# Fold of Wq and Wk by block products, three more two-level products, and modifier's first layer summed in PSUM

## Chip, cores and metric

The kernel runs on one core of one Trainium2 chip, in float32. The metric is the device time of one execution in microseconds (us). A core has a matrix engine (TensorE, PE in the profile, with PEld for its weight loads), a vector engine (VectorE, DVE), a scalar engine (ScalarE, ACT), a general one (GpSimd, POOL) and a queue engine (SyncE, SP) that issues transfers. Each has a queue of its own and works through it in order. Matmuls write to PSUM, which has eight banks of 128 x 512 floats; SBUF holds all else.

## The reference

Four sequences x of 512 tokens and 512 features go through attention, two multilayer perceptrons and a small adapter. Cut to what is computed:

```python
q, k, v = x @ Wq, x @ Wk, x @ Wv
attn = softmax(q @ k.T * 512 ** -0.5)
attn_out = (attn @ v) @ Wp + bp
cms_out = gelu(attn_out @ cW1 + cb1) @ cW2 + cb2 + one_hot(codes)   # 512 -> 2048 -> 512
modifier = gelu(concat(attn_out, cms_out) @ mW1 + mb1) @ mW2 + mb2  # 1024 -> 2048 -> 512
h = clip(x + cms_out + modifier, 0, 1)
up = gelu(h @ W_down[s] + b_down[s]) @ W_up[s] + b_up[s]            # 512 -> 256 -> 512, s by sequence
out = layernorm(h + up) * ln_w[s] + ln_b[s]
```

## The kernel before

**Folded weights.** x Wq (x Wk)ᵀ is x (Wq Wkᵀ) xᵀ, so the kernel first makes w_qk = Wq Wkᵀ and, during the first attention, w_vp = Wv Wp. Wq and Wk are transposed by PE (`transposed`, L409, matmuls L414), copied out of PSUM in turn by DVE (L107) and ACT (L111), and multiplied by `product` (L423, matmuls L428): 16 matmuls of 512 columns. `block_weights` (L449) also makes the sums of w_qk's blocks on DVE as the products end.

**Block products.** Everything behind the fold is multiplied in the form of Strassen and Winograd: of a product of 2 x 2 blocks only seven block products are made instead of eight, from sums of blocks of either operand. They are numbered 1 to 7; a left operand has the sums s1 to s4, a right one t1 to t4. At one level a product saves an eighth of PE's columns; at two levels each of the seven is again made of seven, and another eighth goes. What it costs are additions of results on DVE. Two helpers do these:

- `seven` (L554) keeps the sums in PSUM: products 1, 5 and 6 open banks, 7 and 4 go on accumulating onto the bank of 6, 3 onto the one that DVE's sum y was written to, 2 onto that of 1. In between DVE adds in place (`add`, L509, instruction line L510), so PE waits for DVE inside one group: product 7 waits for `add(y, x, c15)`, product 4 for `add(v, x, c15)`. ACT copies product 1 out as c1 (L575).
- `inner` (L847) gives every product a bank of its own; ACT copies the first (L871), and DVE adds each of the other six out of PSUM (`plus`, L864), seven additions in all.

**Stages.** Sequences go in two pairs. A pair goes through attention (`small_product` L657 with matmuls L664, `pair_product` L595 with matmuls L600), through cms' first layer (`c1_layer`, L1000) and second layer (`second_layer`, L1154, matmuls L1180), through modifier's first layer (`m1_layer`, L1081, matmuls L1096) and second layer, and the adapters. Pair 0's adapters (matmuls L1279, L1288, L1300) are made in steps between the products of pair 1's cms first layer; pair 1's are made in its last layer and behind it. In cms' first layer products 1 and 5 are at two levels (`c1_two_level`, L955, matmuls L979), the other five at one (matmuls L1030). In modifier's first layer all are at two, by `inner`, in two halves g of the output, with `combine_first` (L898) adding the outer seven together on DVE and calling gelu. Both second layers are at two levels, by `inner`.

**Sums of operands.** The inner sums of token operands (`token_sums` L183, instruction line L190, four subtractions a product) are DVE's, made one product ahead. The sums of weights are POOL's: `expansion` (L355) and `late_expansion` (L368) load weights, add blocks (L178 to L181, L298) and store the sums to memory; SP's queue fetches them again into four weight slots, `wslot`. The main program calls a few steps of these generators between products (`steps`, L402), so POOL goes through them in that order, ahead of PE. Late expansion, for modifier's second layer, runs beside pair 0's modifier first layer, two steps per product.

**Small constants.** `constants` (L485 to L505) turns codes and adapter numbers into a one-hot column table (`target`) and row numbers for the gathers (`ex`, `idx_d`, `idx_u`): some 36 DVE instructions of 1 to 8 elements a partition, called in the first attention after w_vp.

**Order.** A scheduler orders the instructions of each engine by the kernel's dependences and a model of their costs; those in `tc.keep_in_program_order` stay in the order of the program on their engine. `second_operands` (L1121) makes the outer sums of a second layer's operand (2048-element subtractions on DVE) as the first layer ends.

## Time and profile before

| | us |
|---|---|
| three runs, median (lowest to highest) | 1199.15 (1198.18 to 1199.61) |
| the profiled execution | 1199.55 |
| its span | 1197.8 |
| PE busy / idle in the span | 1173.2 / 24.6 |
| DVE busy | 891.0 |
| ACT busy | 292.5 |
| POOL busy | 475.3 |

The stages by PE's work in that span: fold 0 to 25.2, attention of pair 0 to 147 and of pair 1 to 255.4, cms' first layer of pair 0 to 348.2 and second to 433.0, modifier's first layer to 606.8 and second to 691.4; then the same for pair 1: 816.6, 901.2, 1070.7 and 1163.9, and the last adapters to 1197.8. The mean granted clock of PE is 0.994.

In the lists of the trace a line such as `PE sum L664 <- DVE sum L510: 4.1, 1, 4.1` reads: PE, at line 664, waited for DVE's line 510, 4.1 us in all, once, the longest 4.1. In the order of time a line has its start, its length, the engine, the line of the kernel, the operation, its output and inputs, and the count of records. A float32 matmul leaves two records.

### The profile page before, as it was taken

To read this page: it belongs to the slowest core of one execution; us is meant where nothing else is said; L and a number is where in the kernel's file an instruction comes from. 1 tells how busy PE (TensorE), PEld (TensorE's weight loads), DVE (VectorE), ACT (ScalarE), POOL (GpSimd) and SP (SyncE) were. 2 spreads that over 40 slices of the span, in tenths; PEclk is the share of its full clock that TensorE was granted. 3 is DMA by queue.
4 is the path that set the end of the run, shared out by engine and by line. 5 is a ranking of instruction groups with operands and counts; after the bars stand their busy time and mean duration, and the time that the engine had idled before them with its cause. 6 is when DMAs were issued, how large, how long until landed. Compare 5 with 4: busy or idle time off the path is not lost.

```text
span 1197.8 us, 13100 instructions
## 1 busy us (share of the span) xinstructions
PE 1173.2 (98%) x4785; PEld 893.2 (75%) x4785; DVE 891.0 (74%) x1234; ACT 292.5 (24%) x535; POOL 475.3 (40%) x517
## 2 busy tenths in 40 slices
PE   8989999999999999999999999999999999999996
PEld 5468548747468888878888857447888888888872
DVE  2755565477789867798799837679895588699947
ACT  3215234426520000012210037461000002230014
POOL 5779999988910048880000532210000010124015
PEclk9999999999999999999999999999999999999998
DMA  8844586699636587886747553142744454675601
GB/s 299 298 154 176 192 321 235 220 386 369 259 111 242 179 276 306 298 287 228 233 163 282 185 184 132 44 141 106 279 143 172 180 206 172 211 245 183 231 1 70
DMA packets 78368, 251.50 MB, mean 210 GB/s; under 512 B 7348, under 2 KB 34016, under 8 KB 63456
## 3 DMA queue, kind: packets, MB, share of 16 engines
q1 hardware_dynamic: 54768, 149.96, 35.4%
q0 software_dynamic: 20736, 89.17, 21.2%
q10 hardware_dynamic: 2800, 11.54, 2.4%
q8 instruction: 38, 0.62, 0.2%
q14 instruction: 26, 0.21, 0.1%
HBM read 185.63 MB, written 65.01 MB: 209 GB/s over the span
## 4 chain that ended last, share of the span: by engine, by line
PE 92%; DVE 5%; ACT 1%; issue 1%; DMA 0%; DVEq 0%
PE i L1180 28%; PE i L1096 26%; PE c L1030 11%; PE sum L600 8%; PE sum L664 7%; PE sum L979 3%; PE prod_ps L428 2%; PE down_ps L1288 2%; PE tr_ps L414 2%; PE up_ps L1300 2%; DVE slot L190 1%; DVE hidden L510 1%; PE res_ps L1279 1%; DVE part L864 1%; DMA wide<-in_L_cond_Wq 0%
## 5 line engine op out<-in xcount | busy, mean ns | idle before, releaser
L1096 PE MATMUL i<-slot,wslot 128*128 128x256 f32 x1184 | 262.0, 380 | 2.3 <-DVE part L864 2.3
L1096 PEld LDWEIGHTS i<-slot,wslot 128*128 128x128 f32 x1184 | 225.1, 190 | 33.6 <-issue 2.4
L1180 PE MATMUL i<-slot,wslot 128*128 128x256 f32 x896 | 202.5, 379 | 0.0
L1180 PEld LDWEIGHTS i<-slot,wslot 128*128 128x128 f32 x896 | 170.4, 190 | 23.0
L871 ACT COPY first<-i 128x256 f32<-128x256 f32 (+1 forms) x56 | 26.8, 478 | 540.4 <-PE i L1180 280.7
L1180 PE MATMUL i<-hidden,wslot 128*128 128x256 f32 x576 | 132.2, 379 | 0.0
L864 DVE TENSOR_TENSOR part<-i,part 128x512 f32<-128x512 f32 (+1 forms) x156 | 90.9, 591 | 42.9 <-PE i L1096 26.2
L1180 PEld LDWEIGHTS i<-hidden,wslot 128*128 128x128 f32 x576 | 109.6, 190 | 16.0 <-issue 1.4
L893 ACT ACTIVATE hidden<-hidden,bias 128x512 f32<-128x512 f32 x128 | 85.2, 716 | 69.6 <-DVE hidden L510 69.5
L1030 PE MATMUL c<-slot,wslot 128*128 128x512 f32 x224 | 97.3, 592 | 0.0
L1030 PEld LDWEIGHTS c<-slot,wslot 128*128 128x128 f32 x224 | 42.5, 190 | 53.1 <-issue 50.4
L1251 POOL DMA_INDIRECT slot<-in_L_cond_W_down,idx_d x12 | 15.4, 1283 | 149.8 <-PE i L1180 88.5
L1251 POOL DMA_INDIRECT slot<-in_L_cond_b_up,idx_e x3 | 4.3, 1423 | 174.1 <-PE i L1096 173.5
L190 DVE TENSOR_TENSOR slot<-hidden,slot 128x1024 f32<-128x1024 f32 x48 | 58.4, 1218 | 0.3
L190 DVE TENSOR_TENSOR slot<-hidden 128x1024 f32<-128x1024 f32 x48 | 58.4, 1217 | 0.0
L864 DVE TENSOR_TENSOR part<-i,first 128x512 f32<-128x512 f32 (+1 forms) x62 | 36.3, 588 | 29.1 <-PE i L1096 16.6
L510 DVE TENSOR_TENSOR sum<-sum,wslot 128x512 f32<-128x512 f32 x48 | 33.4, 697 | 32.5 <-PE sum L600 17.6
L664 PE MATMUL sum<-hidden,wslot 128*128 128x256 f32 x224 | 53.1, 389 | 4.1 <-DVE sum L510 4.1
L510 DVE TENSOR_TENSOR hidden<-c,hidden 128x512 f32<-128x512 f32 x64 | 43.4, 688 | 15.5 <-PE c L1030 14.3
L284 POOL DMA_DIRECT2D slot<-in_L_cond_mW x24 | 17.9, 751 | 90.2 <-DVE slot L190 89.2
L664 PEld LDWEIGHTS sum<-hidden,wslot 128*128 128x128 f32 x224 | 43.4, 195 | 10.5 <-DVE sum L510 4.5
L510 DVE TENSOR_TENSOR hidden<-part,hidden 128x2048 f32<-128x2048 f32 x20 | 47.4, 2370 | 0.5
(301 smaller groups left out, 1990.5 us busy)
## 6 DMA issues: line engine op xcount, KB each, us to landing
wslot<-m_kept SPq DMA_DIRECT2D x48, 1024.0 KB, 6.5
wslot<-m_kept SPq DMA_DIRECT2D x36, 512.0 KB, 4.7
wslot<-c_kept SPq DMA_DIRECT2D x16, 1024.0 KB, 6.3
slot<-in_L_cond_mW POOLq DMA_DIRECT2D x24, 512.0 KB, 7.6
wslot<-in_L_cond_mW SPq DMA_DIRECT2D x24, 512.0 KB, 6.7
slot<-in_L_cond_cW POOLq DMA_DIRECT2D x16, 512.0 KB, 5.4
wslot<-in_L_cond_cW SPq DMA_DIRECT2D x32, 256.0 KB, 4.9
m_kept<-wide POOLq DMA_DIRECT2D x6, 1024.0 KB, 7.0
```

The costliest lines, as they stand in the source:

```text
L190: i = eng.tensor_tensor(out_, one, two, ALU.subtract)
L414: nc.tensor.transpose(ps[d][:, c * P : (c + 1) * P], get(c)[:, d * P : (d + 1) * P], ident)
L510: nc.vector.tensor_tensor(dst, a, b, ALU.add)
L600: nc.tensor.matmul(ps, lhsT=lhs[p][:, c, r * P : (r + 1) * P], rhs=rhs[p][:, c, :], start=(first_ and c == 0), stop=(c == 1), skip_group_c ...
L664: nc.tensor.matmul(v[:, j, :], lhsT=lhs[p][:, c, j * P : (j + 1) * P], rhs=rhs[p][:, c, :], start=(first_ and j == 0 and c == 0), stop=(c ...
L864: nc.vector.tensor_tensor(dst, ps, other, ALU.add)
L871: nc.scalar.copy(c1, p1)
L893: nc.scalar.activation(block[:, t, :], block[:, t, :], AF.Gelu, bias=bias_c[:, 8 * half + t : 8 * half + t + 1],)
L979: nc.tensor.matmul(halves_of(ps)[:, j, :], lhsT=a[g][:, at_[q], j * P : (j + 1) * P], rhs=rhs[q][:, 0, :], start=(first_ and j == 0), stop ...
L1030: nc.tensor.matmul(ps, lhsT=lhs(c, t), rhs=one_level[p][:, c, :], start=(c == 0), stop=(c == 1),)
L1096: nc.tensor.matmul(out_ps[:, j, :], lhsT=a[j][q][:, c, :], rhs=now[q][:, c, :], start=(c == 0), stop=(c == 1),)
L1180: nc.tensor.matmul(ps[:, :256], lhsT=a[k // 2][q][:, k % 2, :], rhs=now[q][:, k, :], start=(k == 0), stop=(k == 3),)
```

## The change

1. The fold of Wq and Wk goes from `product` to `small_product` (28 matmuls of 256 columns, `folded`). The sums of the operands' blocks are made by DVE from the transposes in PSUM (`left_from_psum`, `right_from_psum`), and ACT makes all copies of the transposes. It works in `wslot[0]`, `wslot[1]` and `slot[0]`.
2. `constants` goes from DVE to POOL, between the first weights' expansion and the rest; three gathers of adapter biases, which need it, stand behind it in POOL's queue.
3. In the last pair's cms first layer products 2, 6 and 7 are also at two levels. Their weight sums are made by POOL at the end of late expansion (`expand_c1_late`), the inner sums of their operands and two of the outer additions by POOL too. The steps of pair 0's adapters are called inside the products (`beside`) instead of between them. Late expansion goes at three steps per product.
4. Modifier's first layer goes from `inner` and `combine_first` to `seven`, with the outer additions of each product in its `keep`.
5. `second_operands`, except for pair 0's cms layer: half of the first outer sum is made by ACT copies with a factor of −1 and a transfer that POOL issues and that adds to what stands at its destination (`accum_op`), and one subtraction goes from the first layer's end to the second layer's start.

```diff
@@ late_expansion
-        yield from expand_all(m2_units, slot[6:8], (flat(mod[0]), flat(mod[1]), slot[0]), None)
+        spaces = (flat(mod[0]), flat(mod[1]), slot[0])
+        quarters = lambda tiles: [t[:, at : at + 1024] for t in tiles for at in (0, 1024)]
+        begin, rest = expand_c1_late(quarters(slot[6:8]), quarters(spaces[:2]))
+        yield from expand_all(m2_units, slot[6:8], spaces, None, begin)
+        yield from rest
@@ expand_c1_late, for units (p, u) of p in (2, 6, 7), u in 0, 1
+                weight_sums(
+                    raw[:, 0, 0], raw[:, 0, 1], raw[:, 1, 0], raw[:, 1, 1],
+                    *(to[:, k] for k in range(4)),
+                )
+                if i + 4 < len(units):
+                    load(i + 4)
+                nc.gpsimd.dma_start(out=c1_inner[p, u], in_=sums[i % 4])
+                yield
@@ expansion
         yield from expand_c1(1, lambda: load_raw(cW2, False, 0, slot[4:6]))
+
+        constants()
@@ constants
-            nc.vector.tensor_scalar(target[:, b, :], pos, code[:, b : b + 1], None, ALU.is_equal)
-            nc.vector.tensor_add(target[:, b, :], target[:, b, :], cb2_c)
+            nc.gpsimd.tensor_scalar(target[:, b, :], pos, code[:, b : b + 1], None, ALU.is_equal)
+            nc.gpsimd.tensor_add(target[:, b, :], target[:, b, :], cb2_c)
...
@@ the fold
-    transposed(chunks(wq), big[4])
-    transposed(chunks(wk), big[5])
-    lhs_qk = block_weights(chunks(big[4]), chunks(big[5]), w_qk, slot[0])
+    wq_t, wk_t, s_q, t_k = big[4], big[5], sums_in(wslot[0]), sums_in(wslot[1])
+    transposed(chunks(wq), wq_t, left_from_psum(wq_t, s_q))
+    transposed(chunks(wk), wk_t, right_from_psum(wk_t, t_k))
+    lhs_qk = folded(left_operand(wq_t, s_q), right_operand(wk_t, t_k), w_qk, sums_in(slot[0]))
+    def folded(lhs, rhs, w, s):
+        s1, s2, s3, s4 = (s[:, k] for k in range(4))
+        held = []
+        def keep(half, columns, ps):
+            dst = w[:, 2 * half : 2 * half + 2, 256 * columns : 256 * columns + 256]
+            nc.scalar.copy(dst, ps)
+            if (half, columns) == (1, 1):
+                held.append(ps)
+            elif (half, columns) == (0, 1):
+                minus(s3, w[:, 0:2, :256], ps)
+                minus(s2, held[0], s3)
+                add(s1, held[0], w[:, 0:2, 256:])
+            elif (half, columns) == (1, 0):
+                minus(s4, ps, s2)
+        small_product(lhs, rhs, keep)
+        return left_operand(w, s)
@@ c1_two_level, keep
+            if p == 2:
+                nc.scalar.copy(h11, z)
+            elif p == 1:
+                nc.scalar.copy(h21, z)
+                add(h11, z, h11)
+            elif p == 5:
+                nc.scalar.copy(h22, z)
+            else:
+                add(h21, z, h21)
+                nc.gpsimd.tensor_tensor({6: h12, 7: h22}[p], h22, h21, ALU.add)
...
+        then = {6: [beside], 7: [beside], 4: [beside]} if beside is not None and p != 2 else None
+        seven(2, matmuls, keep, (1, 5, 6, 2, 7, 3, 4), then, at=mod[0])
@@ c1_layer
-            if p in (1, 5):
-                c1_two_level(p, h, two_level[p])
+            if p in two:
+                if more or p == 1:
+                    prepare(two.index(p) + 1)
+                c1_two_level(p, h, ready[p], beside if more else None)
@@ m1_layer
-                inner(matmuls, [[v[:, :, o, t, :] for t in range(2)] for o in range(2)], 256)
-                combine_first(p, h, tiles, part, mb1_c)
+                    if p == 1:
+                        nc.scalar.copy(h11, ps)
+                    elif p == 5:
+                        nc.scalar.copy(h22, ps)
+                    elif p in (6, 7):
+                        dst = {6: h12, 7: h22}[p]
+                        add(ps, ps, {6: h11, 7: h21}[p])
+                        add(dst, ps, h22)
+                        nc.scalar.copy(h21, ps)
+                    else:
+                        dst = {2: h11, 3: h12, 4: h21}[p]
+                        add(dst, ps, dst)
+                    if p in DONE and place in ((0, 1), (1, 0)):
+                        at, half = DONE[p]
+                        gelu(h[at], half, mb1_c, [4 * g + 2 * j + o for j in range(2)])
+                seven(1, matmuls, keep, (1, 5, 6, 2, 7, 3, 4), at=part)
@@ second_operands, after
-            if (p, g) == (3, 1):
-                differences(1, LOW)
-                differences(3, LOW)
+            if (p, g) == (3, 0) and not busy:
+                for two in (slice(0, 2), slice(2, 4)):
+                    tc.keep_in_program_order(
+                        nc.scalar.activation(t1[:, two, :], h11[:, two, :], AF.Copy, scale=-1.0)
+                    )
+            elif (p, g) == (3, 1):
+                if busy:
+                    differences(1, LOW)
+                    differences(3, LOW)
+                else:
+                    nc.gpsimd.dma_start(out=t1[:, LOW, :], in_=h12[:, LOW, :], accum_op=ALU.add)
@@ the pairs
-        for _ in c1_layer(h, c1_rhs, made[2]):
-            steps(between, 2)
+        for _ in c1_layer(h, c1_rhs, made[2], final, lambda: steps(extra, 1)):
+            if not final:
+                steps(between, 2)
@@ beside modifier's first layer
-                steps(between, 2)
+                steps(between, 3)
```

## The prediction

> **What bounds the kernel now.** I read the page's chain first, then the waits of TensorE, then its work in order of time around each wait.
>
> ```profile
> PE 92%; DVE 5%; ACT 1%; issue 1%; DMA 0%; DVEq 0%
> ```
> ```profile
> PE tr_ps L414 <- DMA wide<-in_L_cond_Wq: 4.8, 1, 4.8
> PE sum L664 <- DVE sum L510: 4.1, 1, 4.1
> PE i L1096 <- DVE part L864: 2.3, 2, 2.0
> PE sum L979 <- DVE sum L510: 0.9, 1, 0.9
> PE sum L664 <- ACT wslot L575: 0.8, 2, 0.4
> PE prod_ps L428 <- DVE hidden L107: 0.5, 1, 0.5
> ```
> PE is busy 1173.2 of 1197.8 us. Its idle time is 24.6 us: 13.4 in the list and 11.4 (with rounding) in the last adapters' tail, which the change leaves alone. So time comes off in two ways only: fewer columns through PE, or one of these waits. Nothing that DVE, ACT or POOL saves counts unless a wait ends on it.
>
> The price of a product by level, from PE's work in order of time (start, us, xcount of records; a matmul leaves two):
> ```profile
> 255.40 13.90 PE L1030 MATMUL c<-slot,wslot 128*128 128x512 f32 x32
> 269.13 1.89 PE L979 MATMUL sum<-slot,wslot 128*128 128x256 f32 x8
> ...
> 293.31 13.90 PE L1030 MATMUL c<-wide,wslot 128*128 128x512 f32 x32
> ```
> One product at one level takes 269.13 − 255.40 = 13.73 us; two at two levels take 293.31 − 269.13 = 24.18, 12.09 each. Each product turned saves 1.64.
>
> The first attention's wait:
> ```profile
> 73.93 1.89 PE L664 MATMUL sum<-hidden,hidden 128*128 128x256 f32 x8
> 79.93 5.41 PE L664 MATMUL sum<-hidden,wslot 128*128 128x256 f32 x16 [4.11 <-DVE sum L510]
> 85.18 3.62 PE L664 MATMUL sum<-hidden,hidden 128*128 128x256 f32 x16
> ```
> PE stands 4.11 us, and its next 16 records then take 5.41 instead of the 3.62 of any other 16. DVE is in the constants (L487 to L505) from 70.57 to 78.40, and its two sums for PE stand behind them. The same matmuls of pair 1 need 17.81 us (178.87 to 196.68), here 23.87 (68.75 to 92.62).
>
> Then by stage (columns: busy of PE, PEld, DVE, ACT, POOL, granted clock, DMA):
> ```profile
> 433.00:606.80 173.80, 171.53 (x786) 150.01 (x785) 138.13 (x140) 26.00 (x42) 83.54 (x85) 0.99 0.78 270
> 901.20:1070.70 169.50, 169.50 (x786) 148.97 (x785) 118.49 (x140) 26.11 (x42) 15.03 (x11) 1.00 0.58 197
> 515.00:545.00 30.00, 27.73 (x120) 23.48 (x119) 29.69 (x25) 3.79 (x7) 18.19 (x19) 0.94 0.85 296
> ```
> modifier's first layer of pair 1 is PE without a gap. Pair 0's takes 4.3 us more: 2.27 idle, and 27.73 × 0.06 = 1.7 of lower clock around it. There POOL works beside it, and these DVE instructions, alone of their kinds, are stretched:
> ```profile
> 457.83 6.01 DVE L190 TENSOR_TENSOR slot<-slot,slot 128x512 f32<-128x512 f32 x1
> ...
> 531.40 0.68 DVE L864 TENSOR_TENSOR part<-i,first 128x512 f32<-128x512 f32 x1
> 532.00 3.47 DVE L190 TENSOR_TENSOR slot<-cms,slot 128x512 f32<-128x512 f32 x1
> 535.39 0.68 DVE L864 TENSOR_TENSOR part<-i,part 128x512 f32<-128x512 f32 x1
> 535.99 0.67 DVE L190 TENSOR_TENSOR slot<-cms 128x512 f32<-128x512 f32 x1
> ```
> L190, both operands in SBUF, takes 0.67 or 3.47; L864, one of them in PSUM, always 0.68. PE's 2.0 us wait ended at the L864 behind the 3.47.
>
> **The change, part by part.**
>
> *Constants to POOL: −6.1.* DVE's queue ahead of the two sums empties, and this stretch becomes pair 1's: 23.87 − 17.81 = 6.06. POOL gets 25 instructions of a few elements and, earlier than before, three gathers. No such instruction stands in its rows; its tensor_tensor rows (0.70 at 256 elements, 1.26 at 512, 2.34 at 1024) run to about 0.15 at zero. 25 × 0.15 + 3 × 0.97 = 6.7, less a wait of 3.69 on a transfer that POOL now spends in part on them: about +3; with tiny ones at 0.3, +7. Behind them in its queue stand the whole later weight expansion and x1's sums (101.07 to 111.04). PE wants those from 116.95, 13 us after the tightest of them; it now comes 6.6 earlier (with the fold), which leaves 6.4 to 7. Nothing waits up to there; at +10 it would be 3 and a clock loss of 1.8. I take 0.
>
> *Fold of Wq and Wk: −0.5.* Sixteen 512-column matmuls (13.73) become 28 of 256 (12.09). But ACT now makes all eight copies: from 9.34 at 0.53 each the first left operand is there at about 12.5 instead of 11.24. 12.55 + 12.09 = 24.65 against 25.2. DVE's 16 subtractions of 256 columns run beside it; the operands wanted third and fourth are ready at my count some 2 us early. Behind it, w_qk's last sum stands in DVE's queue after the bias copy, and PSUM banks for x1's transposes wait for it: up to +1. The 1.75 us gap on PE (10.8 to 12.55) adds clock: see below. Ends −1.6 and +2.5.
>
> *Cms' first layer, last pair: −3.4.* Products 2, 6, 7: 3 × 1.64 = −4.92. The new weights are made by POOL in late expansion: 6 × (4 × 0.70 + 2 × 0.6) = 24 us from about 535 to 560, wanted at 700. Inner sums and the 16 adds of 512 columns (20 us) go to POOL, which works only 25.6 of that stage's 125 us; the sums are wanted 10 us and more after they can be made. What can cost: adapters' steps now stand inside products. A step waits for an ACT square root, whose table loads are 1.28 each, and takes PSUM banks, all eight of which a two-row product uses. Before, one such place cost 0.87 (L979 behind two 1.04 us adapter instructions on DVE). Ends 0 and 5 for six such places; I take two at 0.75: +1.5.
>
> *modifier's first layer: 0 in pair 0, +0.65 in pair 1.* Matmuls and columns stay. Before, DVE took each product out of PSUM, 7 adds per inner block; now 4 to 5 adds remain in PSUM's chain, and PE itself waits for two of them: product 7 accumulates onto the bank of 6 after DVE's y has read it, and product 4 onto the same bank after v has. An inner product is 4 matmuls, 1.73 us; an add 0.69. So y has about 2 us to spare and v 2.3 to 3.6, with L190's four 512-wide sums between them in DVE's queue. At 0.67 nothing is late. Ahead of the last block's chain stand four 1024-wide L190 (4 × 1.22), and y is done 7.5 us after that product against 6.9 wanted: +0.65 in either pair. In pair 0 the 2.27 + 1.7 of before go with their L864, but stretched L190s return at the new places. With before's durations in the new order, four of them cost 0.9, 1.2, 1.3 and 1.7 with some clock; they need not fall there again, and half of this is 2.6, with 1.7 of clock. Gone 4.0, come 4.3, less what the idle DVE catches up: 0, ends −4.5 and +12.
>
> The rule here is the Trainium skill's "SBUF — State Buffer", Who interferes with whom: DVE and GpSimd share a port pair, a DVE instruction with two SBUF inputs is locked out for the length of one GpSimd instruction, and one with a single SBUF input is not. It speaks against this change, which lengthens POOL's work in the stage by 24 us. The trace agrees on which are hit. It differs on how far: POOL's instructions beside the 3.47 were 0.56 to 0.74 long, so the rule would make an L190 at most about 0.67 + 0.74 = 1.4, within every margin, and the pair 4 us faster, 1186 in all; the row has 3.47 and 6.01. I go by the row.
>
> Of a gap's clock the skill's "TensorE: Matmul & The Clock Gate", Part 1, says that the rate halves after an idle window of about 3.4 us. By it the 4.11 costs its 1.8, as the row has it, but a 2.0 gap nothing, and the fold's 1.75 nothing. The 515 to 545 row has 0.94 after gaps of 2.27. By the row the new stalls cost up to 1.7 together, as summed above; for the fold I leave up to 1 in its bound.
>
> *Second layers: 0.* Half of the first sum leaves DVE (2.28) for two ACT copies and an accumulating transfer from POOL, which has products of 12 us for its 7; another difference (2.28) moves to the layer's start, less 1.6 saved there, against a margin of 3.0 for the banks. Without that cover, +3.
>
> Sum: −6.1 − 0.5 − 3.4 + 0 + 0.65 = −9.35. Profiled execution 1199.55 (span 1197.8 and 1.75 around it), so 1190.2; the median shown is 0.4 lower: 1190.
>
> **Rivals.**
> - All waits stay hidden: −6.1 − 1.6 − 4.9 − 4.0 = −16.6, about 1182.5. For it: PSUM-sourced adds never stretched, and DVE has less to do. Against it: the four L190s.
> - The last pair's gain is eaten by adapters inside products: +3.4, 1193.5. For it: the 0.87. Against it: a step per product is thin.
> - POOL delays x1's sums: from 7 us of delay PE stops at L664; at 10, 3 + 1.8: 1195. Against it: 6.4 of margin.
> - Slower: product 4 or 7 of modifier's first layer stands behind a stretched L190 in most of pair 0's five later products while POOL works. Twelve such places at 1.0 with a clock share of 0.4 each are 16.8 for the 4 gone, which ends near 1203 with the rest unchanged; it decides from 13 us of such waits. For it: 6.01 and 5.21 are in the trace. Against it: a third of L190s were stretched, most fall in the loose places.
>
> **How the numbers follow.** As summed 0.52 (own range 1186 to 1194), all hidden 0.14, adapters 0.14, POOL 0.08, slower 0.12. A run of this kernel tells about 0.2%, 2.4 us: faster is below 1196.8. The first four are (0.88, less 0.03 of their upper ends), the slower one is nearly all above 1201.5 (0.10). Same 0.05. Left out at 1182.5 and 1199 are half of the second and most of the last: 0.18.
>
> **What would show it.** Right: L664 without a wait near 75; first products at 12.5; L979 with five products in the last pair and waits under 2 us; modifier's L1096 counterpart in pair 1 at 170. Wrong: PE waits on DVE sums above 5 us between 433 and 607, clock under 0.97 there, POOL's x1 sums later than 113, or new waits for ACT or banks from 690 to 810.

## The result and the profile after

The changed kernel takes 1194.88 us in the median of ten executions (1192.39 to 1197.95), the kernel before 1199.41 beside it (1195.35 to 1200.96): a ratio of 0.9965, 95% interval 0.9953 to 0.9976. That is 4.2 us less by the ratio (4.5 by the medians), where 9.15 were forecast. The time lies between 1182.5 and 1199, the ends that the prediction named, but above the 1186 to 1194 of its likeliest case: the direction holds, and in this set less than half of the forecast gain came. A second set of executions, beside another set of the kernel before, gave 1192.30, ratio 0.9939 (0.9922 to 0.9956), or 6.3 us less by the medians; so the size of the gain is known to some 2 us only.

The profiled execution has a span of 1192.5 us (1194.29 with what lies around it). Its waits of PE (us in total, times, longest), to be read against the list of before:

```profile
PE tr_ps L466 <- DMA wide<-in_L_cond_Wq: 4.5, 1, 4.5
PE sum L1204 <- DVE sum L555: 4.3, 5, 1.1
PE sum L1061 <- DVE sum L555: 1.3, 1, 1.3
PE sum L645 <- DVE sum L555: 0.9, 1, 0.9
...
PE sum L1061 <- ACT mod L620: 0.7, 1, 0.7
PE sum L709 <- ACT hidden L691: 0.7, 1, 0.7
PE sum L1061 <- DMA wslot<-c_inner: 0.4, 1, 0.4
PE sum L709 <- POOL wslot L180: 0.4, 1, 0.4
```

The 4.1 us behind the constants and their slow clock are gone: the 16 records that took 5.41 take 3.62, with no wait ahead of them. PE's timeline of the changed kernel (start and length in us, operation, count):

```profile
73.58 1.89 PE L709 MATMUL sum<-hidden,hidden 128*128 128x256 f32 x8
75.30 3.62 PE L709 MATMUL sum<-hidden,wslot 128*128 128x256 f32 x16
78.75 3.62 PE L709 MATMUL sum<-hidden,hidden 128*128 128x256 f32 x16
```

In their place stand small waits, on DVE, ACT, POOL and transfers. Two layers stand out: cms' first layer of pair 0, whose code does the same products as before, and modifier's first layer, in either pair. The stages of after (columns as in the prediction, with GB/s as the last), from cms' and modifier's first layer of pair 0 to those of pair 1:

```profile
249.84:344.26 94.42, 93.31 (x274) 51.51 (x272) 72.25 (x87) 45.53 (x76) 81.16 (x95) 1.00 0.84 317
428.87:603.20 174.33, 170.67 (x786) 148.46 (x785) 113.69 (x137) 46.84 (x78) 97.90 (x124) 1.00 0.88 311
687.80:808.84 121.04, 119.64 (x442) 80.55 (x441) 82.80 (x137) 65.54 (x102) 55.16 (x54) 1.00 0.45 151
893.44:1063.93 170.49, 169.75 (x786) 148.80 (x785) 94.47 (x137) 46.88 (x78) 13.11 (x12) 1.00 0.60 202
```

From the starts of the stages in the two profiles, the sum against the forecast:

| part of the span | before | after | difference | forecast |
|---|---|---|---|---|
| PE's start | 4.78 | 4.49 | −0.29 | – |
| start to w_vp's product | 50.24 | 50.17 | −0.07 | −0.5 |
| first softmax | 27.86 | 21.80 | −6.06 | −6.06 |
| the mix of x1's sums | 30.69 | 31.55 | +0.86 | 0 |
| cms' first layer, pair 0 | 92.84 | 94.42 | +1.58 | 0 |
| modifier's first layer, pair 0 | 173.74 | 174.33 | +0.59 | 0 |
| cms' first layer, pair 1 | 125.24 | 121.04 | −4.20 | −3.4 |
| modifier's first layer, pair 1 | 169.45 | 170.49 | +1.04 | +0.65 |
| from the last up-projections to the end | 34.09 | 35.35 | +1.26 | 0 |
| all others | | | 0 | 0 |
| sum | 1197.8 | 1192.5 | −5.3 | −9.3 |

### The profile page after: what moved, and what is told of

It reads as the page before. It is cut to its first block, busy times and chain, and to the rows that moved or that the text cites. A ratio compares the mean times of both kernels' runs of the same rounds, so it can differ in the third digit from the quotient of the medians.

```text
span 1192.5 us, 13488 instructions
## 1 busy us (share of the span) xinstructions
PE 1165.8 (98%) x4881; PEld 908.0 (76%) x4881; DVE 841.7 (71%) x1218; ACT 330.5 (28%) x600; POOL 532.7 (45%) x619
## 3 DMA queue, kind: packets, MB, share of 16 engines
q1 hardware_dynamic: 55600, 153.11, 35.4%
## 4 chain that ended last, share of the span: by engine, by line
PE 47%; DVE 2%; issue 1%; ACT 0%; DVEq 0%; ACTq 0%
PE i L1322 21%; PE sum L1204 14%; PE sum L1061 5%; PE down_ps L1430 2%; PE c L1136 2%; PE up_ps L1442 2%; PE res_ps L1421 1%; DVE slot L190 0%; DVE sum L555 0%; DVE hidden L1450 0%; DVE stats L1452 0%; ACT wide L1275 0%; DVE hidden L1474 0%; DVE hidden L1463 0%; DVE cms L555 0%
## 5 line engine op out<-in xcount | busy, mean ns | idle before, releaser
L1204 PE MATMUL sum<-slot,wslot 128*128 128x256 f32 x1184 | 264.7, 380 | 4.3 <-DVE sum L555 4.3
L1204 PEld LDWEIGHTS sum<-slot,wslot 128*128 128x128 f32 x1184 | 224.5, 190 | 36.8 <-DVE sum L555 6.5
L1322 PE MATMUL i<-slot,wslot 128*128 128x256 f32 x896 | 202.5, 379 | 0.0
L1322 PEld LDWEIGHTS i<-slot,wslot 128*128 128x128 f32 x896 | 170.2, 190 | 23.1
L555 DVE TENSOR_TENSOR sum<-sum,part 128x512 f32<-128x512 f32 x84 | 58.6, 697 | 71.2 <-PE sum L1204 70.5
L555 DVE TENSOR_TENSOR hidden<-sum,hidden 128x512 f32<-128x512 f32 x112 | 75.8, 687 | 24.7 <-PE sum L1204 10.7
L1136 PE MATMUL c<-slot,wslot 128*128 128x512 f32 x160 | 69.2, 592 | 0.0
L190 DVE TENSOR_TENSOR slot<-hidden,slot 128x1024 f32<-128x1024 f32 x48 | 59.2, 1233 | 0.4
L190 DVE TENSOR_TENSOR slot<-hidden 128x1024 f32<-128x1024 f32 x48 | 59.4, 1238 | 0.0
L1061 PE MATMUL sum<-mod,wslot 128*128 128x256 f32 x224 | 52.3, 380 | 1.7 <-DVE sum L555 1.3
L555 DVE TENSOR_TENSOR part<-sum,part 128x512 f32<-128x512 f32 x28 | 19.3, 689 | 47.4 <-PE sum L1204 39.8
L1061 PEld LDWEIGHTS sum<-mod,wslot 128*128 128x128 f32 x224 | 42.3, 190 | 8.1 <-DVE sum L555 1.7
```

The lines of the kernel that those rows point to most:

```text
L190: i = eng.tensor_tensor(out_, one, two, ALU.subtract)
L555: nc.vector.tensor_tensor(dst, a, b, ALU.add)
L1061: nc.tensor.matmul(halves_of(ps)[:, j, :], lhsT=a[g][:, at_[q], j * P : (j + 1) * P], rhs=rhs[q][:, 0, :], start=(first_ and j == 0), stop ...
L1136: nc.tensor.matmul(ps, lhsT=lhs(c, t), rhs=operands[p][:, c, :], start=(c == 0), stop=(c == 1),)
L1204: nc.tensor.matmul(v[:, j, :], lhsT=a[j][q][:, c, :], rhs=now[q][:, c, :], start=(first_ and j == 0 and c == 0), stop=(c == 1), skip_group ...
L1322: nc.tensor.matmul(ps[:, :256], lhsT=a[k // 2][q][:, k % 2, :], rhs=now[q][:, k, :], start=(k == 0), stop=(k == 3),)
```

## The experiments

Every kernel below was timed beside the kernel before on the same chip; the ratio is to that. Stage lengths are from the profile of one execution of each: "fold" is from PE's start to w_vp's product, "softmax" the stretch with the constants, c0 and c1 cms' first layer of pair 0 and 1, m0 and m1 modifier's, "tail" the stretch from the last up-projections to the end. A stage length is that of one execution: changed and after_again are the same program, and differ by 0.4 to 1.1 us in the fold, m0 and c0 and by 2 in c1.

| kernel | median us | ratio (95%) | fold | softmax | c0 | m0 | c1 | m1 | tail |
|---|---|---|---|---|---|---|---|---|---|
| before | 1199.41 | 1 | 50.24 | 27.86 | 92.84 | 173.74 | 125.24 | 169.45 | 34.09 |
| changed | 1194.88 | 0.9965 (0.9953–0.9976) | 50.17 | 21.80 | 94.42 | 174.33 | 121.04 | 170.49 | 35.35 |
| after_again | 1192.30 | 0.9939 (0.9922–0.9956) | 50.62 | 21.81 | 95.54 | 173.62 | 119.09 | 170.49 | 35.40 |
| const_in_gap | 1189.86 | 0.9925 (0.9906–0.9944) | 50.62 | 21.80 | 94.10 | 174.50 | 119.09 | 170.49 | 34.95 |
| const_on_dve | 1199.67 | 1.0007 (0.9996–1.0018) | 50.85 | 31.67 | 92.84 | 174.05 | 119.10 | 170.50 | 35.36 |
| constants_alone | 1190.20 | 0.9932 (0.9916–0.9948) | 49.92 | 21.79 | 92.84 | 170.93 | 125.24 | 169.39 | 33.96 |
| psum_sums_alone | 1207.99 | 1.0078 (1.0056–1.0100) | 50.01 | 31.10 | 92.84 | 173.86 | 125.24 | 171.35 | 34.09 |
| psum_sums_and_constants | 1198.35 | 0.9998 (0.9988–1.0008) | 50.86 | 21.79 | 92.84 | 175.15 | 125.24 | 171.56 | 33.94 |
| m1_by_inner | 1201.73 | 1.0012 (0.9992–1.0032) | 52.88 | 21.80 | 93.88 | 184.71 | 119.09 | 171.72 | 35.32 |
| m1_and_sums_old | 1202.88 | 1.0018 (1.0001–1.0034) | 50.16 | 21.80 | 95.36 | 183.20 | 119.09 | 171.69 | 35.28 |
| m1_and_all_sums_old | 1194.56 | 0.9973 (0.9958–0.9988) | 50.88 | 21.80 | 95.37 | 170.84 | 123.05 | 169.64 | 35.17 |
| c1_last_old | 1199.08 | 1.0002 (0.9989–1.0014) | 53.09 | 21.80 | 94.36 | 177.44 | 124.05 | 170.49 | 34.29 |
| c1_two_level_alone | 1187.29 | 0.9903 (0.9890–0.9916) | 50.84 | 21.80 | 92.84 | 173.12 | 119.09 | 169.21 | 35.12 |
| c1_two_level_spread | 1188.33 | 0.9907 (0.9889–0.9925) | 50.03 | 21.80 | 92.84 | 174.00 | 119.09 | 169.22 | 35.14 |
| gap_old_fold | 1192.61 | 0.9931 (0.9913–0.9949) | 49.62 | 21.80 | 93.56 | 178.88 | 119.09 | 170.49 | 35.39 |
| gap_and_early_table | 1190.68 | 0.9936 (0.9917–0.9955) | 49.59 | 21.80 | 95.01 | 173.28 | 119.10 | 170.49 | 34.89 |
| fold_alone | 1191.27 | 0.9940 (0.9927–0.9953) | 51.39 | 21.80 | 94.95 | 171.72 | 125.25 | 169.22 | 33.98 |
| fold_phase | 1190.16 | 0.9930 (0.9918–0.9943) | 49.34 | 21.80 | 95.39 | 173.93 | 119.10 | 170.50 | 34.94 |
| best_of_parts | 1190.51 | 0.9934 (0.9918–0.9950) | 49.74 | 21.80 | 95.53 | 174.97 | 119.10 | 169.21 | 35.27 |

### The constants

> The changed kernel with the small constants issued on POOL earlier, in the wait of 6.45 us that POOL has there before its third group of first-layer weight sums. Theory (the constants cost POOL 7.1 us of delay, and that delay is what comes back on PE later): POOL's sums of x1 start near 101.5 instead of 108.15, the PE wait on POOL at 121 goes, cms' first layer of pair 0 falls from 94.4 to 92.8 us because POOL's stores no longer meet the weight fetches; span 2.4 us below the changed kernel's, some 1192 in all. Rival (those 1.6 us in cms' first layer come from the reordered weight loads of the expansion, or from chance): the stage stays at 94.4 and only 0.9 is gained.

```diff
         then()
+        if u == 0:
+            constants()
         outer = c1_outer[u]
...
-        constants()
         yield from expand_all(
```

In the changed kernel POOL's constants and gathers took 9.5 us (58.04 to 67.6), less the 3.7 us wait that they filled, and POOL came to them 1.3 us later than to the same place in before; x1's sums start at 108.15 instead of 101.07, 7.1 us later and not 3. Tiny instructions are not all at 0.15 us, as POOL's timeline shows (the bracket is the idle time before and its releaser):

```profile
58.46 1.13 POOL L539 TENSOR_SCALAR target<-pos,code 128x4 f32<-128x4 f32 x4
...
61.55 0.59 POOL L551 TENSOR_SCALAR idx_d<-pos,ex_v 128x4 int32<-128x4 f32 x2
...
63.93 1.14 POOL L1393 DMA_INDIRECT bd<-in_L_cond_b_down,idx_u  x1 [0.15 <-POOL idx_u L552]
65.38 0.96 POOL L1393 DMA_INDIRECT bd<-in_L_cond_b_down,idx_u  x1 [0.30 <-issue]
```

Those with a scalar operand take 0.28 to 0.30, casts and additions 0.13 to 0.16 from start to start, 0.23 in the mean of the 25; and a gather has 0.3 us of issue before it. Moved into the wait, the constants leave x1's sums at 104.65, and the wait on POOL goes (30.69 instead of 31.55; in after_again it was only 30.86). But c0 stays at 94.1: the rival was right there, POOL's delay does not make that stage longer. The median is 2.4 us under the second set of the changed kernel, by intervals that overlap.

> The changed kernel with the small constants back on DVE at their old place. Theory: the first attention's wait of 4.1 and its slow clock return (+6.06), the 0.86 and 1.58 us lost behind POOL's delay go: +3.6 against the changed kernel, some 1198.5. Rival (the delay of POOL costs nothing): +6.1, some 1201.

```diff
-        nc.gpsimd.tensor_copy(pos, pos_i)
+        tc.keep_in_program_order(nc.vector.tensor_copy(pos, pos_i))
...
             lhs_vp = block_weights(chunks(wv_t), chunks(wp), w_vp, slot[2])
+            constants()
```

The median is 4.8 us above the first set of the changed kernel and 7.4 above the second, so theory and rival are not told apart by it. In the profile x1's wait and the extra time in c0 are gone, as the theory has it. But the softmax stretch is 31.67, longer than the 27.86 of before, with a PE wait of 6.95 instead of 4.11. The same happens in psum_sums_alone (31.10), whose fold and constants are those of before. DVE's timeline in psum_sums_alone, with POOL at work beside it:

```profile
70.62 2.00 DVE L492 TENSOR_SCALAR target<-pos,code 128x4 f32<-128x4 f32 x2
72.54 0.15 DVE L493 TENSOR_TENSOR target<-target,bias 128x4 f32<-128x4 f32 x1
72.61 1.86 DVE L492 TENSOR_SCALAR target<-pos,code 128x4 f32<-128x4 f32 x1
74.39 0.15 DVE L493 TENSOR_TENSOR target<-target,bias 128x4 f32<-128x4 f32 x1
74.46 0.22 DVE L492 TENSOR_SCALAR target<-pos,code 128x4 f32<-128x4 f32 x1
```

The same instruction takes 0.22 or 1.86 us. How many are stretched differs between the profiles of the same code: PE's wait behind them is 4.1 us in before and 6.2 in psum_sums_alone. So 6.06 was the price in one profiled execution; what the median one pays, no profile shows.

> The kernel before with one part of the change alone: the small constants on POOL, in its wait ahead of the third group of first-layer sums. Theory (6.06 us go at the first attention, and PE, that much earlier beside transfers that come no earlier, gives 1 to 2.5 of it back in cms' first layer of pair 0 on weight fetches): first attention 21.8 us, cms' first layer of pair 0 93.8 to 95.3 instead of 92.8; in all 4 to 5 below before. Rival (the fetch waits there come from other parts of the change): the stage stays at 92.84 and the whole is 6 below before.

```diff
 (kernel before)
-        tc.keep_in_program_order(nc.vector.tensor_copy(pos, pos_i))
+        nc.gpsimd.tensor_copy(pos, pos_i)
...
         then()
+        if u == 0:
+            constants()
```

This one part takes 8.0 us off (0.9932), as much as the whole change or more. c0 is 92.84 with PE 6.7 us earlier than before, so coming earlier alone does not bring the fetch waits; the rival was right. And m0 falls to 170.93 by itself, a stage in which no line was changed (its row, columns as above):

```profile
426.14:597.07 170.93, 169.48 (x785) 148.88 (x784) 134.82 (x139) 26.11 (x42) 83.34 (x85) 1.00 0.78 274
```

The clock is 1.00, and PE's one listed wait there is 1.45 us on a fetch. DVE's stretched subtractions are still there (5.96 and 3.83 us), but PE no longer stands behind one. So before's 2.0 us stall depended on which subtraction was stretched, and when; what changed that here was not looked into.

### The sums in PSUM

> The kernel before with one part alone: modifier's first layer with its sums in PSUM. Theory (PE waits for DVE in the last block, +1.04 in pair 1; in pair 0 waits of 2 to 3 us take the place of the 2.3 and the slow clock of before): pair 1 170.5, pair 0 172.5 to 174.5; POOL's expansion in pair 0 ends earlier than 536 because DVE reads two SBUF operands at once less often; 0 to 1 above before. Rival (the lighter DVE pays by itself): pair 0 below 172, the whole 1 or more below before.

> The kernel before with the constants in POOL's earlier wait and modifier's first layer with its sums in PSUM, all else as before. Theory (the layer costs by itself, through PE's waits for DVE and for L190 stretched by POOL): pair 0 173.5 to 174.5 against 170.9, pair 1 170.5 to 171.4 against 169.4; 4 to 5 above the constants alone, 1194.5. Rival (with POOL's work as short as before, the lighter DVE keeps up): pair 0 171.5 or less, no more than 2 above, 1191.5.

```diff
 (kernel before; in the second with the constants moved as above)
-                inner(matmuls, [[v[:, :, o, t, :] for t in range(2)] for o in range(2)], 256)
-                combine_first(p, h, tiles, part, mb1_c)
+                seven(1, matmuls, keep, (1, 5, 6, 2, 7, 3, 4), at=part)
```

Beside the constants alone, which it differs from in this layer only, the second takes 8.2 us more in the median. Between the profiled executions it is 7.3: 4.2 and 2.2 in the two stages, and 0.9 in the fold, whose code is the same. That is on the theory's side and above its 4 to 5. psum_sums_alone lies even 9.8 above before, where 0 to 1 was expected; in its profile 3.2 are the dearer constants of the softmax stretch and 1.9 the stage of pair 1, and the rest of the median is not in the profile (1204.28, near the lowest of its runs). PE's waits in pair 0 of psum_sums_and_constants (start of what came after the wait, then its length in brackets):

```profile
459.60 12.35 PE L1097 MATMUL sum<-slot,wslot 128*128 128x256 f32 x56 [1.28 <-DVE sum L510]
472.55 29.62 PE L1097 MATMUL sum<-slot,wslot 128*128 128x256 f32 x136 [0.59 <-DVE sum L510]
529.03 1.13 PE L1097 MATMUL sum<-cms,wslot 128*128 128x256 f32 x4 [1.82 <-DMA wslot<-in_L_cond_mW]
583.90 12.35 PE L1097 MATMUL sum<-slot,wslot 128*128 128x256 f32 x56 [0.22 <-DVE sum L510]
596.94 5.45 PE L1097 MATMUL sum<-slot,wslot 128*128 128x256 f32 x24 [0.68 <-DVE sum L510]
```

Ahead of the first stands the stretched subtraction, again 6 us long, and the PSUM addition that PE wants stands behind it (DVE's timeline of the same kernel):

```profile
452.05 6.08 DVE L190 TENSOR_TENSOR slot<-slot,slot 128x512 f32<-128x512 f32 x1
458.06 0.68 DVE L510 TENSOR_TENSOR part<-sum,part 128x512 f32<-128x512 f32 x1
458.84 0.70 DVE L510 TENSOR_TENSOR sum<-sum,part 128x512 f32<-128x512 f32 x1
```

In before's profile the same 6 us at 457.8 cost PE nothing. The wait of 1.82 on a fetch need not be this layer's: constants_alone has one of 1.45, a block product later. In pair 1 the last block waits 0.68, as worked out; 0.22 on DVE and 0.65 on a fetch come besides. A wait costs more than it lists, since a group's record ends later than the next group starts (1.89 us long, 1.73 from start to start): in the changed kernel pair 1 lists one wait, of 0.67, which moves PE by 0.83; a pause of 0.24 ahead of 1031.81 is too short for the list, and the stage is 1.04 longer than before.

> The changed kernel with modifier's first layer as it was, each product added out of PSUM by DVE. Theory (the sums kept in PSUM make PE wait where the old way did not): modifier's first layer of pair 1 falls from 170.5 to 169.5 us, pair 0 from 174.3 to 173.7; together 1.6 below the changed kernel, 1193.3. Rival (the lighter DVE pays in pair 0, where POOL now works 24 us longer): pair 0 rises to 177 or more, the whole is 2 us slower than the changed kernel.

> The changed kernel with modifier's first layer as it was, as in the run before, and also without the ACT copies and the adding transfer of the second layers' sums (all on DVE again). Theory A (the 12.5 us wait of that run came from the adding transfer, 1024 KB that POOL's queue moves at some 210 GB/s while weight fetches stand behind it): the wait goes, modifier's first layers are 173.7 and 169.5, 1.6 below the changed kernel, 1193. Theory B (the 24 us of weight sums and their transfers that POOL has more in that stage are enough to hold the old form back): pair 0 stays above 176, and the whole is slower than the changed kernel.

> The changed kernel with modifier's first layer as it was, and now without the ACT copies and the adding transfer for both second layers of both pairs (the run called the same before had left modifier's own adding transfer in: its edit reached only cms' layer). Theory A (POOL ends its longer work near 564 beside the old layer, not near 552, so its two adding transfers of x fall on the last weight fetches whether or not the third is there): pair 0 stays above 176, with a PE wait on a fetch of modifier's weights between 575 and 590. Theory B (only the third adding transfer makes three in 9 us): the wait falls under 2 us, pair 0 near 174, pair 1 169.5, the whole 1 to 2 below the changed kernel.

```diff
-                seven(1, matmuls, keep, (1, 5, 6, 2, 7, 3, 4), at=part)
+                inner(matmuls, [[v[:, :, o, t, :] for t in range(2)] for o in range(2)], 256)
+                combine_first(p, h, tiles, part, mb1_c)
...
-        made = second_operands(h, pair == 0)     (the second and the third)
+        made = second_operands(h, True)
...
-        made = second_operands(h)                (the third)
+        made = second_operands(h, True)
```

With the old layer inside the changed kernel, pair 0 takes 184.7 us, as the rival of m1_by_inner had it, though not for its reason: 12.5 of it is one wait on a fetch of modifier's weights. PE's line and the window around it in m1_by_inner (clock, DMA share and GB/s are the window's last three columns):

```profile
587.88 2.47 PE L1225 MATMUL i<-slot,wslot 128*128 128x256 f32 x5 [12.54 <-DMA wslot<-in_L_cond_mW]
575.00:590.00 15.00, 2.46 (x7) 1.80 (x6) 2.98 (x2) 0.00 (x0) 0.00 (x0) 0.66 1.03 262
```

POOL's transfers ahead of it, and SP's fetch of those weights, in their timelines:

```profile
562.41 1.47 SPq L434 DMA_DIRECT2D wslot<-in_L_cond_mW  x2
564.75 0.57 POOL L282 DMA_DIRECT2D c_inner<-mod  x1 [0.30 <-POOL mod L181]
565.58 0.91 POOL L1528 DMA_DIRECT2D cms<-xT_kept  x1 [0.26 <-issue]
571.40 0.85 POOL L1283 DMA_DIRECT2D wide<-hidden  x1 [4.92 <-ACT wide L1276]
573.91 0.85 POOL L1528 DMA_DIRECT2D cms<-xT_kept  x1 [1.65 <-PE i L1225]
```

Three transfers of 1024 KB that add to what is there are issued within 9 us. The two fetches of 512 KB that PE stands for were issued ahead of all three, at 562.4 and 563.3, and land 25 and 26 us later; in before the same two take 6 and 8 us. The transfer engines' account from 572 to 582, by queue (q0 is POOL's, q1 SP's; packets, MB, share of the engines' time):

```profile
q0 software_dynamic: 266, 1.93, 92.9%
q1 hardware_dynamic: 286, 0.31, 10.8%
```

The two queues get about as many packets each. But POOL's are mostly of 8 KB and SP's mostly of 1 KB, so SP's queue moves a sixth of the bytes that POOL's moves. And an adding packet of 8 KB takes 0.63 us of an engine in this stretch, where a plain one took 0.35 in before (545 to 556).

In before the two adding transfers of x stand 24 us apart (556.9 and 581.2), and the third does not exist. m1_and_sums_old still had the third, since its edit did not reach modifier's layer: 183.2. Without it, and without the ACT copies that go with it, the wait is gone and the stages are 170.84 and 169.64, theory B of that run; so the third adding transfer, part 5 of the change, is what the old layer could not stand. The median is still only that of the changed kernel, and its executions spread from 1190.4 to 1201.8.

In the changed kernel the three are at 552.3, 570.8 and 576.8. POOL's last store of sums is at 550 there, beside the old layer at 559 to 566: the same 120 POOL instructions are busy for 98 us there and for 113 in m1_by_inner, where sixteen of the 256-element additions take more than 0.8 us, up to 2.8. The layer with sums in PSUM has fewer DVE instructions with two SBUF operands, which fits, but was not varied alone. That is what the layer gives. It counts beside part 3's POOL work and part 5's third transfer; without that transfer the old layer is as fast in the median (1194.56).

### The fold

> The changed kernel once more, for a second profile of it. If the fold's 50.2 us of the first profile was a lucky start (ACT's copies of the transposes wait behind a Wv load that its queue issues, 7.7 us in that profile and up to 8.9 in others), the start stage is above 50.5 here, and above 52.5 when PE's gap before the fold passes 1.9 us; cms' first layer of pair 0 is again 1 to 1.6 us above 92.8, and modifier's first layers are again near 174.3 and 170.5. If the profile's stage lengths are fixed, all are within 0.3 of the first.

```diff
 (no edit: the changed kernel)
```

The fold is 0.45 us longer in the second profile, c0 1.1 longer, m0 0.7 shorter and c1 1.95 shorter; m1 and the tail are the same. So the lengths are not fixed, and c0 is longer than before in both.

> The changed kernel with the constants in POOL's earlier wait and the fold of Wq and Wk as it was, 16 matmuls of 512 columns. Theory (the new fold gains 1.6 us of columns and loses it to ACT's copies, DVE's chain and, in some runs, the clock): the start stage is 50.2 us; within 1 us of the kernel with the new fold, 1190, and less spread between runs. Rival (the new fold pays its 0.5 or more): 0.5 to 1.5 us slower, 1191.

> The kernel before with the constants in POOL's earlier wait and the new fold of Wq and Wk, all else as before. Theory (columns -1.6, ACT's eight copies +1.3, DVE's chain +0.9, the clock in some runs +1.5, the turned quarters +1 to 1.6 in cms' first layer of pair 0): start 50.2 to 53.1 against 49.9, that stage 93.8 to 94.5; in all 1 to 3 above the constants alone, 1192. Rival (the fold gains 0.5 as forecast): 1189.7.

```diff
 (gap_old_fold: const_in_gap with)
-    lhs_qk = folded(left_operand(wq_t, s_q), right_operand(wk_t, t_k), w_qk, sums_in(slot[0]))
+    lhs_qk = block_weights(chunks(big[4]), chunks(big[5]), w_qk, slot[0])
 (fold_alone: the reverse, in constants_alone)
```

With the new fold the stretch to w_vp's product was 50.2 to 53.1 us in the nine profiles that have it without the early table load; with the old one 49.6 to 50.9 in seven. What moves it is ACT's queue: it issues the loads of Wv, and the second of them waits for an earlier transfer; only then come the table load and eight copies. The timeline of all engines in the changed kernel:

```profile
5.79 1.90 ACTq L120 DMA_DIRECT2D slot<-in_L_cond_Wv  x2
7.72 1.28 ACT L731 ACT_TABLE_LOAD   x1 [7.72 <-DMA wide<-in_L_cond_Wk]
...
11.61 2.05 PE L709 MATMUL sum<-hidden 128*128 128x256 f32 x8 [0.71 <-ACT hidden L691]
```

And in c1_last_old, where load, copies and PE all come 1.2 us later:

```profile
5.70 3.21 ACTq L120 DMA_DIRECT2D slot<-in_L_cond_Wv  x2
8.94 1.28 ACT L730 ACT_TABLE_LOAD   x1 [8.94 <-DMA wide<-in_L_cond_Wk]
...
12.83 3.58 PE L708 MATMUL sum<-hidden 128*128 128x256 f32 x8 [2.17 <-ACT hidden L690]
```

The granted clock between 12 and 18 us is 0.72 in c1_last_old and m1_by_inner (gaps of 2.17 and 1.92), and 1.00 in all others (gaps of 0.35 to 1.70, and one of 2.12 soon after a short wait).

fold_alone has c0 at 94.95; constants_alone, which differs in the fold only, has 92.84. PE's waits in that stage of fold_alone:

```profile
265.23 1.10 PE L1015 MATMUL sum<-slot,wslot 128*128 128x256 f32 x4 [0.33 <-DMA wslot<-in_L_cond_cW]
268.50 2.83 PE L1015 MATMUL sum<-mod,wslot 128*128 128x256 f32 x12 [1.30 <-DMA wslot<-c_inner]
```

The changed kernel waits at the same two places (0.71, which its list puts down to ACT, and 0.40), constants_alone at neither. Over all profiles, c0 is 93.9 to 95.5 in eleven of the twelve with the new fold (const_on_dve has 92.84), and 92.84 in six of the seven with the old one (gap_old_fold has 93.56). So the fold goes with these waits, 2.1 us here in a stage 200 us behind it and in a kernel that differs in nothing else, but other parts of the change can bring one as well. In all fold_alone is 1.1 us above constants_alone in the median, by intervals that overlap, and 3.6 in these two stretches of the profile, near its theory. gap_old_fold's stretch is 1.0 shorter and its c0 0.5 than const_in_gap's; its median is spoiled by 178.9 us in m0, with a fetch wait of 3.2, and says nothing about the fold.

> The changed kernel with the constants in POOL's earlier wait, and a copy of one column on ACT placed before the second half of the Wv loads, so that ACT's table load of 1.28 us is done before the transposes are there. Theory (the fold now stands behind ACT's queue: load issue, table load, eight copies): copies start 1.28 us earlier, PE's gap before the fold is below 1 us in every run, the clock stays at 1.00 between 12 and 18 us, and the start stage is 49.3 to 50.3 us; 0.5 to 1 us below the kernel with the constants alone, 1189. Rival (DVE's chain of subtractions behind the fold sets the end of that stage anyway): the stage stays above 50.3, no gain.

```diff
+    warm = const.tile([P, 1], F32, name="warm")
+    tc.keep_in_program_order(nc.scalar.copy(warm, ident[:, :1]))
     wv = weight((nc.scalar, nc.scalar), Wv, slot[2])
```

The stretch falls to 49.59, the gap to 0.35, as the theory has it; the whole does not gain against const_in_gap (0.9936 and 0.9925). In the profiles c0 is 0.9 longer here and takes most of it back.

> The changed kernel with constants in POOL's earlier wait, the early table load, and the counter that deals out the quarters of the fourth weight slot turned on by two after the new fold, so that it stands as it did with the old fold. Theory (the last-read quarter is the one that the first fetch of cms' first layer writes, so all three fetches into that slot stand behind it): those fetches are issued 1.3 to 2.5 us earlier, cms' first layer of pair 0 falls from 95.0 to 93.5 us; 1 to 1.5 below the run without it, 1189. Rival: the stage stays at 95, no gain.

```diff
 (gap_and_early_table with)
     lhs_qk = folded(left_operand(wq_t, s_q), right_operand(wk_t, t_k), w_qk, sums_in(slot[0]))
+    temps[0] += 2
```

c0 is 95.39: refuted. The turned quarters do decide when the first of the inner-sum fetches is issued (2.5 us ahead of that stage's start in all kernels with them as before, 0.8 to 1.5 with them turned), and setting them right brings the first back; but the second comes at +1.6, where it was −1.0 to −0.7 in before and constants_alone, and PE waits for it. Over 18 profiles, c0 is 92.84 wherever the second is issued before the stage starts (one more has 92.84 at +1.6), and 93.6 to 95.5 otherwise. The transfer engines are full ahead of the stage with either fold: between 25 and 20 us ahead of it their share is 0.57 in the changed kernel and 0.54 in constants_alone, in the next 5 us 0.85 and 0.97, and from there on 0.98 or more in both. c1_two_level_alone, with the old fold and 92.84, has 0.57 and 0.88, so this does not tell the folds apart. Why the second fetch comes late was not settled.

### The two-level products

> The changed kernel with only two of the seven products of the last pair's cms first layer at two levels, as before, and without the POOL sums made for the others. Theory: that stage rises from 121.0 to 125.2 us (+4.2), and modifier's first layer of pair 0 loses up to 1 us of its waits since POOL stops 24 us earlier there: +3.2 to +4.2 against the changed kernel, 1198.5. Rival (the adapters inside products or the longer POOL work eat most of it): +1 or less.

```diff
-        for _ in c1_layer(h, c1_rhs, made[2], final, lambda: steps(extra, 1)):
+        for _ in c1_layer(h, c1_rhs, made[2], False, None):
...
-        yield from rest
```

> The kernel before with the constants in POOL's earlier wait and the three more two-level products of the last pair (their sums on POOL, the adapters' steps inside products), all else as before (fold, modifier's first layer, second layers' sums). Theory (the products give 6 us in their stage and nothing is lost but in modifier's first layer of pair 0, where POOL now ends near 564 and its two adding transfers of x meet the last weight fetches): last cms first layer 119.1 against 125.2, pair 0 of modifier's first layer 171 in some runs and up to 182 in others, tail 35.2 against 34.0; median 1187 to 1190 with a wide spread. Rival (POOL's extra work costs nothing there): 1184 to 1186, narrow.

```diff
 (const_in_gap with the old fold, the old modifier first layer and all sums of second layers on DVE)
```

c1 is 119.1 in eleven of the profiles: 6.15 less than before, all of the 4.92 and the old 0.87 too. Adapters inside products cost nothing there; the 1.3 us wait of the changed kernel's first profile is not in these, and m1_and_all_sums_old (123.05) has one of 1.99, listed on ACT. c1_two_level_alone is the fastest of all, as its theory has it: 0.9903, 2.9 us below constants_alone. Half of the stage's gain is lost in the profile, in m0 (173.1, a fetch wait of 1.5 beside the adding transfers), in the tail and in the start (50.84 against 49.92, by the same code). c1_last_old agrees with its theory in c1 (+3.0 to +5.0), but its median is also made of a fold with the slow clock and of 177.4 in m0, where PE waits 5.3 us on the sums in PSUM, 3.44 at once.

> The same with the second of the two adding transfers of x held back until the last product of modifier's first layer has begun its activations (a one-column copy of them on POOL ahead of it), some 20 us later. Theory: no PE wait on a weight fetch above 2 us in modifier's first layer of pair 0, which takes 171; median 1185, spread of runs under 4 us. Rival (the waits come from POOL's stores and loads themselves, or the transfer then meets the second layer's fetches): same spread and median as without it, or a longer second layer than 84.6.

```diff
+            if s == 1 and pair == 0:
+                late = small.tile([P, 1], F32, name="late")
+                tc.keep_in_program_order(nc.gpsimd.tensor_copy(late, h[2][:, 0, :1]))
             nc.gpsimd.dma_start(out=cms[s], in_=xT_kept[2 * pair + s], accum_op=ALU.add)
```

The transfer came at 592.7 instead of 570.8, and a PE wait of 2.67 us on a fetch was still there, at 575. Refuted: the second of the two is not needed for it. The fetch was issued at 559.6 and took 15.5 us; beside it stand POOL's last stores and the first adding transfer (563.2), and which of them holds it was not tried.

The tail is 34.9 to 35.4 in every profile with these products and 33.9 to 34.3 in every one without. Its instructions have the same lengths and waits in both; the difference lies between the last output's issue and the end of the span, 5.2 to 5.8 us against 4.4 to 4.7. The cause stays open.

> The changed kernel with the constants in POOL's earlier wait, ACT's table load ahead of the second half of Wv, and modifier's first layer of the last pair as it was (products added out of PSUM, its second layer's sums on DVE), while pair 0 keeps the sums in PSUM. Theory: start 49.6 us, modifier's first layer of pair 1 169.5 instead of 170.5, all else as in the run with the early table; 1 us below that, 1189 to 1189.5. Rival (PE waits on weight fetches in the last pair too): pair 1 above 170.5, no gain.

```diff
 (gap_and_early_table with)
+        layer = m1_layer_inner if final else m1_layer
-        made = second_operands(h)
+        made = second_operands(h, final)
```

m1 is 169.21, 1.3 less, as expected; m0 has 2.2 us on a fetch, and the median is that of gap_and_early_table.

## Why the prediction was right in direction and wrong in size

**The step that failed** is the term of modifier's first layer: "Gone 4.0, come 4.3", taken as 0 in pair 0, and +0.65 in pair 1. The 4.0 were credited to this part, and they were not its to take: the constants' move alone takes 2.8 us off that stage (170.93 against 173.74). What is left of the term is a cost. Beside the constants alone the sums in PSUM made the two stages 4.2 and 2.2 us longer and the median 8.2. In the median the constants' move alone was worth 8.0 us. All the other parts together were forecast at −3.25; by the ratios they gave back 4.0 us of the 8.0 in the first set (0.9965 against 0.9932), and 0.8, within the intervals, in the second (0.9939). Inside the changed kernel the old layer without the third adding transfer has shorter stages in its profile (170.84 and 169.64), but no lower median (1194.56); why not is open.

Against the profile of before, 4.0 us of the forecast are missing. Cms' first layer of pair 0 lacks 1.6, the tail 1.3, modifier's first layers 1.0, the mix 0.9 and the fold 0.4; the last pair's cms layer gave 0.8 more than forecast, and PE started 0.3 earlier. The first two were put at nothing: the one is not named, and of the tail it is said that the change leaves it alone.

*Constants.* The size held to the digit in the profile (6.06), with some luck, since the same instructions cost PE 4.1 us in one profile and 6.2 in another. What was mis-sized is the delay on POOL: 7.1 us where +3 was chosen, because the intercept of big instructions (0.15) was taken for tiny ones (0.23 in the mean), the gathers' issue of 0.3 each was left out, and POOL came 1.3 later. The bound named for that case was right: PE stopped on POOL, for 0.86 in all, and 0.17 in the second profile.

*Fold.* "−0.5" failed too. Its columns are saved, but ACT's copies stand behind a load that waits for an earlier transfer, by an amount that changes between executions, and the forecast took the one table load of before's profile as fixed. Behind it DVE's chain holds PE for 0.88 (L645), inside the +1 that was named. Not seen at all was the longer cms' first layer of pair 0, 1.6 to 2.7 us, which comes with this part in all but one profile.

*Cms' first layer, last pair.* −3.4 forecast, −4.2 and −6.15 measured; the allowance for adapters inside products was not needed. Of the cost on POOL the prediction said that sums are ready long before they are wanted, which is so; it did not ask what POOL's transfers do to the fetches beside them.

*Modifier's first layer, its waits.* These were seen at about their size, of 1.12, 0.63, 1.12 and 0.73, at products 7 and 4 as worked out, and 0.67 in pair 1. The last of the four is the +0.65 "in either pair", which the sum leaves out for pair 0. The other three are 2.9 us where half of four, 2.6, was taken, and that is luck: another profile (c1_last_old) has 1.16, 3.44 and 0.68 in all.

*The rules.* By the rule of the Trainium skill's "SBUF — State Buffer", Who interferes with whom, a DVE instruction with two SBUF inputs is held for one POOL instruction; the rows of after have L190 at 3.19 with POOL's instructions at 0.56 to 0.74 beside it, and 5.92 and 6.08 elsewhere, where one of POOL's beside it is 2.36. The row decides again. Of the clock the row of before was the worse guide: gaps of up to 1.1 us left it at 1.00 throughout modifier's layers, and the 1.7 us put in for it did not come. Gaps of 1.9 and 2.2 at the fold did lower it, short of the 3.4 us window that the skill's "TensorE: Matmul & The Clock Gate", Part 1, gives, and one of 2.1 did not.

*The rivals.* The rival of delayed x1 sums came true at a small size. None of the others did, and transfers colliding with weight fetches, which cost 12.5 us in m1_by_inner and lengthen cms' first layer of pair 0, were not among them.

## What to carry to other kernels

Before counting a stall of one profiled execution as a gain, ask whether another part of the same change, or mere timing, removes it: here one of five parts alone was worth as much as the five together, or more. Where PE is 98% busy and the transfer engines run at 0.8 to 1.0, list the transfers of every queue around each weight fetch, with the size of their packets, as carefully as the instructions; adding transfers above all. An accumulation kept in PSUM makes the matrix engine wait inside a product for a vector engine that used to run a product behind it; here that cost up to 3.4 us in one wait, where a stretched DVE instruction stood ahead of the sum.

## What was not expected of the hardware

A DVE operation on four columns (128x4) took 0.22 or 1.86 us with POOL at work beside it. POOL operations on as few took 0.13 to 0.30 us, where the slope of large ones pointed at 0.15. Three adding transfers of 1024 KB within 9 us kept the transfer engines fully busy at 262 GB/s; their queue and that of the fetches got about as many packets each, of 8 KB and of 1 KB, and ordinary fetches of 512 KB that had been issued ahead of the three took 25 us instead of 6 to 8.
